# A transformer block on one core: values projected for two head groups at once, weights fetched per group, one tile pool for both stages

## The chip, the cores and the metric

The kernel runs on one core of a Trainium2 chip. The core has a matrix engine (TensorE, PE in the profile, with its weight loads shown apart as PEld), three engines for elementwise work (VectorE or DVE, ScalarE or ACT, GpSimd or POOL) and SyncE (SP), whose queue issues most transfers. SBUF is the on-chip memory that the engines read; PSUM is the accumulator that TensorE writes, used here as eight banks of 512 float32 per partition. The metric is the device time of one execution in microseconds, and lower is better.

## The reference

The input is x of 8 sequences x 1024 positions x 512 features in float32. Each sequence goes through attention with 16 heads of 32 features and then through a feed-forward part:

```python
qvk = (layernorm(h) @ Wqvk).reshape(b, s, 3, H, HD)       # 512 -> 3 * 512
q, v, k = qvk[:, :, 0], qvk[:, :, 1], qvk[:, :, 2]
scores = (einsum('bshi,bthi->bsth', q, k) + causal_mask) / sqrt(512)
wv = einsum('bsth,bthi->bshi', softmax(scores, axis=2), v)
x = x + layernorm(wv @ Wo)                                 # the attention's own input is layernorm(x)
hidden = layernorm(x) @ W1 + b1                            # 512 -> 2048
hidden = hidden + quantum_phase * w_imag * sin(theta + hidden * 0.1) * 0.1
x = x + layernorm(relu(hidden) @ W2 + b2)                  # 2048 -> 512
```

`softmax(scores, axis=2)` normalises over the key positions t. Its maximum over them is computed in full by the kernel.

## The kernel before

**Blocks and groups.** One sequence is one block b. A block's attention runs over four head groups g, each of four heads, so 128 columns of queries, keys and values. Then comes the feed-forward part (FFN). Everything is float32 but the maxima, which are split into bfloat16 parts; a float32 matmul shows as two records in the profile.

**One group.** `find_maxima` computes the scores once (L536) only for their row maxima: VectorE drains the PSUM banks with masked minima (L566, since queries carry a minus sign) on the diagonal tiles and with plain reductions (L554) elsewhere. The last two units of this, `MAX_LATE`, are run by `later(at)`, right ahead of the first two key units of the second part. The maxima are split by GpSimd (`split`), transposed on TensorE (the four bfloat16 transposes at L117) and copied to mT by ScalarE (L624). Then `weigh` goes over key units (`KEY_UNITS`): a matmul puts minus the maximum into PSUM (L642), the scores are computed again on top (L653), ScalarE takes the exponential (L668), and GpSimd clears the masked square (L672). `weighted_values` (L691) multiplies with the values one unit later, through `flush`.

**Fill.** TensorE executes in program order. The projections of the *next* group are a Python generator, `project_qkv(b, g)`, that `advance` moves a step at a time between the score units: a step is two matmuls of 512 columns for queries and keys (L437), or eight of 128 columns for values (L458) with one bank and one ScalarE copy (L466). `MAX_FILL` says how many steps follow each of the four runs of `find_maxima`; one more `advance(work)` stands behind the transposes of the maxima, one behind each of the first two key units (`at < 2`), and one at each of the last two. In group 2 the next block's normalised rows are also transposed there (`norm1`), and in group 3 the first half's output projection begins (`finish_block`, L857).

**FFN.** `feed_forward` runs eight steps of products with mixed (sums and differences of) W1 tiles (L949) and accumulates with W2 (L1033). The products "5", "4" and "6" read `mixed`, which GpSimd makes at L893 from the transposed rows. `load_w1(9)` and `load_w2(4)` keep tiles in flight on SP's queue.

**PSUM.** `psum` hands out banks in program order. It prefers the bank, or the pair of banks, that was released longest ago in that order (`done_at`); a tile that is not yet `drained` keeps its bank, and with it the pair that the bank belongs to, out of use. A score unit and a key unit take two pairs each, of the four. Whatever engine read the bank last is waited for by the matmul that writes it next.

**SBUF.** `wqvk_sb` (24 KB per partition) and `wo_sb` (8 KB) stay resident; queries and keys have a pool of 2 (`qkp`), values of 2 (`vp`), scratch of attention and FFN one of 8 (`pp`), W1 tiles 10 and W2 tiles 5. All allocations of a pool are in turn; a new tile waits for the last reader of the one whose place it takes.

Of the kernel before, what the change touches and what calls it, by code (L numbers as in the profile page):

```python
# [32 lines left out]
def kernel(  # L33
# [33 lines left out]
    qkp = ctx.enter_context(tc.tile_pool(name="qkp", bufs=2))  # L67
    vp = ctx.enter_context(tc.tile_pool(name="vp", bufs=2))
    pp = ctx.enter_context(tc.tile_pool(name="pp", bufs=8))
    tmp = ctx.enter_context(tc.tile_pool(name="tmp", bufs=5))  # L70
    small = ctx.enter_context(tc.tile_pool(name="small", bufs=4))
    w1p = ctx.enter_context(tc.tile_pool(name="w1p", bufs=10))
    w2p = ctx.enter_context(tc.tile_pool(name="w2p", bufs=5))
# [55 lines left out]
    wqvk_sb = const.tile([P, KC, 3 * D], F32, tag="wqvk", name="wqvk_sb")  # L129
    wo_sb = const.tile([P, KC, D], F32, tag="wo", name="wo_sb")  # L130
# [8 lines left out]
    for cols in (slice(0, P), slice(P, D)):  # L139
        for part in (0, 1, 2):  # L140
            of = slice(part * D + cols.start, part * D + cols.stop)
            nc.scalar.dma_start(wqvk_sb[:, :, of], wqvk_v[:, :, of])
        if cols.start == 0:
            for t in range(TPB, NT):
                load_x(0, t, nc.scalar)
# [41 lines left out]
    nc.scalar.dma_start(wo_sb, w_o.rearrange("(kc p) n -> p kc n", p=P))  # L187
# [45 lines left out]
    def w1_tile():  # L233
        return w1p.tile([P, 2, 2, P], F32, tag="w1", name="w1_t")
# [189 lines left out]
    def project_qkv(b, g):  # L424
# [3 lines left out]

        qk[b, g] = qkp.tile([P, 2, S], F32, tag="qk", name=f"qk_{b}_{g}")
        v[b, g] = vp.tile([P, NT, P], F32, tag="v", name=f"v_{b}_{g}")  # L430

        def queries_or_keys(n, half):
            pq = psum([P, HALF])
            c0 = 2 * n * D + g * P
            for kc in range(KC):
                in_order(
                    nc.tensor.matmul(  # L437
                        pq,
                        wqvk_sb[:, kc, c0 : c0 + P],
                        xnT[b, half][:, kc, :],  # L440
                        start=(kc == 0),
                        stop=(kc == KC - 1),
                    )
                )
                if kc == 1:
                    yield True
            dst = qk[b, g][:, n, half * HALF : (half + 1) * HALF]
            in_order(nc.scalar.activation(dst, pq, AF.Copy, scale=1.0 if n else -QSCALE))
            drained(pq)
            yield True  # L450

        def values(t0):
            pv = psum([P, 2, P])
            c0 = D + g * P
            for t in (t0, t0 + 1):
                for kc in range(KC):
# [4 lines left out]
                            wqvk_sb[:, kc, c0 : c0 + P],  # L461
# [4 lines left out]
            in_order(nc.scalar.copy(v[b, g][:, t0 : t0 + 2, :], pv))  # L466
            drained(pv)
            yield True

        yield from queries_or_keys(0, 0)  # L470
        yield from values(0)
        yield from queries_or_keys(1, 0)
        yield from queries_or_keys(0, 1)
        yield from queries_or_keys(1, 1)
        for t0 in (2, 4, 6):
            yield from values(t0)
# [13 lines left out]
    MAX_FILL = ((3, 2, 2, 2), (1, 2, 2, 2))  # L490
# [6 lines left out]
    def find_maxima(b, g, work, sums, more):  # L497
# [3 lines left out]
        t = qk[b, g]  # L501
# [23 lines left out]
        def run_unit(pieces):  # L525
# [4 lines left out]
            for i, kc in pieces:  # L530
                k0 = kc * HALF
                n = min(HALF, (i + 1) * P - k0)
                for j in range(HPG):
# [4 lines left out]
                            t[r, 0, i * P : (i + 1) * P],  # L538
                            t[r, 1, k0 : k0 + n],
# [57 lines left out]
        for n, (run, fill) in enumerate(zip(MAX_RUNS, MAX_FILL[g > 0])):  # L597
# [11 lines left out]
        advance(work)  # L609
# [18 lines left out]
    def weigh(b, g, c, keys, mT):  # L628


        t = qk[b, g]
# [3 lines left out]
        for kb in keys:  # L635
# [14 lines left out]
            for j in range(HPG):  # L650
# [4 lines left out]
                        t[r, 1, kb * P : (kb + 1) * P],  # L655
                        t[r, 0, q0 : q0 + n],
# [74 lines left out]
    def attention(b, wvT, after):  # L731
# [16 lines left out]
        def projections(g):  # L748
            if g + 1 < NG:
                return project_qkv(b, g + 1)  # L750
            if g + 1 == NG and b + 1 < B:
                return project_qkv(b + 1, 0)
            return iter(())

        work = projections(0)
        for g in range(NG):
            more, first = after(g)
# [3 lines left out]
            for c in range(2):  # L761
# [3 lines left out]
                for u, keys in enumerate(units):  # L765
                    later(at)
                    weights, placed = weigh(b, g, c, keys, mTs[c])
                    if at < 2:
                        advance(work)
# [6 lines left out]
                    if c and u == len(units) - 2:  # L776
                        finish(work)
                        work = projections(g + 1)
                    if c and u >= len(units) - 2:
                        advance(work)  # L780
# [42 lines left out]
            flush()  # L823
            if g == NG - 1:
# [4 lines left out]
        return more  # L829

    def finish_block(b, half, wvT, x2T, mixed):
# [21 lines left out]
        def project(t):  # L853
            y = psum([P, D])
            for kc in range(KC):
# [4 lines left out]
                        wo_sb[:, kc, :],  # L860
# [41 lines left out]
    def feed_forward(b, x2T, mixed, before, between):  # L902
# [22 lines left out]
        def load_w2(depth):  # L925
            while len(w2_ahead) < depth and w2_next[0] < 4 * STEPS:
                t = w2p.tile([P, D], F32, tag="w2", name="w2_t")
# [161 lines left out]
        for s in range(STEPS + 1):  # L1089
            if s == NSTEP:  # L1090
# [3 lines left out]
            for n in range(4):  # L1094
# [4 lines left out]
                advance(rest)  # L1099
                if s > 0:  # L1100
# [6 lines left out]
    first_norm, work = norm1_first(), project_qkv(0, 0)  # L1107
    advance(first_norm, TPB + 4)
    for _ in range(TPB):
# [3 lines left out]
    advance(work, 4)  # L1113
    prepare_parameters()
    finish(work)
    rest = iter(())
    for b in range(B):
        load_tables()
        wvT = [tp.tile([P, KC, HALF], F32, tag="t", name=f"wvT_{b}_{n}") for n in range(2)]
        x2T, mixed = {}, {}  # L1120

        def after(g, b=b, wvT=wvT, x2T=x2T, mixed=mixed, rest=rest):
# [10 lines left out]
            if g == NG - 1:  # L1133
                return finish_block(b, 0, wvT[0], x2T, mixed), len(KEY_UNITS[0]) + 1
            return iter(()), 0

        before = attention(b, wvT, after)
        rest = feed_forward(b, x2T, mixed, before, finish_block(b, 1, wvT[1], x2T, mixed))
# [44 lines left out]
```

## Time and profile before

| what | value |
|---|---|
| median of 3 runs | 3766.18 us (3761.59 to 3766.65) |
| the profiled execution | 3764.15 us, of which the span is 3762.4 us |
| TensorE busy | 3697.7 us, 98% of the span |
| granted TensorE clock, mean | 0.994 |
| one block (stretch 977 to 1441) | 464 us, TensorE busy 460.07 |
| DMA | 267.12 MB, mean 71 GB/s |

The profile is of one execution, so what is added up from its rows belongs to 3764.15 us and not to the median. A group of instructions is shown by its line, engine, operation and tiles; the numbers are busy time and the mean of one instruction. Matmuls overlap in the pipeline, so the mean of one is longer than the step from one start to the next; for what a stretch of matmuls costs, the chain of work that ended last is the better view, since each piece there lasts until the next begins. A wait is listed with what released it: total, number of times, longest.

### The profile page before, as it was taken

The numbers are of one execution on the slowest core, as the hardware profiler recorded it, in microseconds if no ns is written. First come the engines' busy times: TensorE is split into PE (matmuls) and PEld (weight loads), VectorE is DVE, ScalarE is ACT, GpSimd is POOL, SyncE is SP. The second block draws the span as 40 slices with busy tenths as digits, with TensorE's granted clock in tenths as the row PEclk, the third lists the DMA queues.
The fourth block names the chain that finished last, engine by engine and source line by source line (L and its number), as shares of the span: only waits on it lengthen the run. The fifth ranks groups of instructions, "written<-read, shape, count | busy, mean of one in ns | idle before, by whom it ended". The sixth has DMA issues, their size and how long they took to land.

```text
span 3762.4 us, 55976 instructions
## 1 busy us (share of the span) xinstructions
PE 3697.7 (98%) x21185; PEld 2062.4 (55%) x21185; DVE 2486.1 (66%) x5355; ACT 1417.1 (38%) x2704; POOL 650.7 (17%) x1204
## 2 busy tenths in 40 slices
PE   7999999999999999999999999999999999999998
PEld 4446655466554664446644466444664456654565
DVE  4866567666676666766577665776667765677655
ACT  3562135511465114651146411564115641156310
POOL 3212012120212102121022110221102211022200
PEclk9999999999999999999999999999999999999999
DMA  7003420044200442004420044100441003400132
GB/s 247 26 10 107 134 82 13 4 117 132 73 15 4 122 133 68 12 7 126 134 60 12 12 129 133 53 13 18 131 133 46 13 21 112 131 29 1 40 111 77
DMA packets 152909, 267.12 MB, mean 71 GB/s; under 512 B 16256, under 2 KB 27584, under 8 KB 152640
## 3 DMA queue, kind: packets, MB, share of 16 engines
q1 hardware_dynamic: 148368, 258.31, 23.2%
q10 hardware_dynamic: 4272, 5.24, 0.4%
q8 instruction: 167, 2.74, 0.3%
q14 instruction: 102, 0.84, 0.1%
HBM read 239.37 MB, written 24.12 MB: 70 GB/s over the span
## 4 chain that ended last, share of the span: by engine, by line
PE 95%; ACT 2%; DVE 1%; POOL 1%; DMA 0%; issue 0%; ACTq 0%; POOLq 0%; SPq 0%; DVEq 0%
PE banks L1033 23%; PE banks L949 20%; PE banks L437 12%; PE banks L536 8%; PE banks L691 7%; PE banks L653 7%; PE banks L458 7%; PE banks L857 6%; PE banks L642 3%; PE banks L117 2%; PE banks L706 1%; ACT w L668 1%; POOL mix L893 0%; ACT x2T L305 0%; DMA wqvk_sb<-in_L_attn_Wqvk_dram 0%
## 5 line engine op out<-in xcount | busy, mean ns | idle before, releaser
L1033 PE MATMUL banks<-w_t,hid 128*128 128x512 f32 x2048 | 915.5, 592 | 0.0
L668 ACT ACTIVATE w<-banks 128x1024 f32<-128x1024 f32 (+1 forms) x640 | 565.7, 936 | 291.9 <-PE banks L653 291.9
L1033 PEld LDWEIGHTS banks<-w_t,hid 128*128 128x128 f32 x2048 | 387.2, 190 | 393.0 <-issue 376.9
L720 DVE TENSOR_TENSOR w<-w 128x1024 f32<-128x1024 f32 (+3 forms) x400 | 408.6, 1062 | 200.8 <-PE banks L691 157.8
L566 DVE CUSTOM_DVE_ANT_0 es<-banks,mask 128x128 f32<-128x128 f32 (+3 forms) x1024 | 433.0, 486 | 104.6 <-PE banks L536 104.6
L437 PE MATMUL banks<-xnT,wqvk_sb 128*128 128x512 f32 x1024 | 481.6, 609 | 6.5 <-ACT xnT L305 6.5
L972 ACT ACTIVATE u<-u 128x1024 f32<-128x1024 f32 x128 | 135.3, 1057 | 903.9 <-DVE u L971 903.9
L949 PE MATMUL banks<-x2T,w_t 128*128 128x256 f32 x2048 | 473.6, 379 | 0.0
L949 PEld LDWEIGHTS banks<-x2T,w_t 128*128 128x128 f32 x2048 | 387.4, 190 | 127.9 <-issue 81.3
L672 POOL TENSOR_SCALAR_AFFINE_SELECT w<-w 128x256 f32<-128x256 f32 x512 | 278.4, 560 | 856.8 <-ACT w L668 814.0
L554 DVE TENSOR_REDUCE mx<-banks 128x1 f32<-128x512 f32 (+1 forms) x384 | 309.8, 862 | 102.0 <-PE banks L536 102.0
L949 PE MATMUL banks<-mix,w_t 128*128 128x256 f32 x1536 | 359.6, 384 | 15.4 <-POOL mix L893 15.4
L949 PEld LDWEIGHTS banks<-mix,w_t 128*128 128x128 f32 x1536 | 294.2, 192 | 86.3 <-issue 30.6
L653 PE MATMUL banks<-qk 32*128 32x512 f32 (+3 forms) x3072 | 330.6, 491 | 0.0
L437 PEld LDWEIGHTS banks<-xnT,wqvk_sb 128*128 128x128 f32 x1024 | 182.5, 190 | 245.1 <-issue 180.9
L691 PE MATMUL banks<-w,v 128*32 128x512 f32 (+3 forms) x3072 | 314.8, 495 | 1.0 <-POOL w L672 1.0
L536 PE MATMUL banks<-qk 32*128 32x512 f32 (+3 forms) x3072 | 313.5, 511 | 0.3 <-DVE mx L566 0.2
L586 ACT ACTIVATE es<-es,mx 128x512 f32<-128x512 f32 (+3 forms) x512 | 279.7, 551 | 2.1 <-DVE mx L566 2.1
L458 PEld LDWEIGHTS banks<-wqvk_sb,xnT 128*128 128x128 f32 x2048 | 239.0, 192 | 50.8 <-issue 23.6
L458 PE MATMUL banks<-wqvk_sb,xnT 128*128 128x128 f32 x2048 | 259.5, 280 | 0.0
L976 DVE SCALAR_TENSOR_TENSOR hid<-u,coef,hid 128x512 f32<-128x512 f32 x256 | 180.9, 749 | 109.7 <-ACT u L972 109.7
L857 PE MATMUL banks<-wo_sb,wvT 128*128 128x512 f32 x512 | 241.4, 612 | 3.2 <-DVE wvT L728 3.2
(110 smaller groups left out, 3173.4 us busy)
## 6 DMA issues: line engine op xcount, KB each, us to landing
w_t<-w_mixed SPq DMA_DIRECT2D x448, 256.0 KB, 2.7
w_t<-in_L_ffn_W_dram SPq DMA_DIRECT2D x256, 256.0 KB, 2.6
xin<-in_L_attn_h_dram SPq DMA_DIRECT2D x112, 256.0 KB, 3.5
out_dram<-x SPq DMA_DIRECT2D x64, 256.0 KB, 2.0
x<-in_L_attn_h_dram SPq DMA_DIRECT2D x60, 256.0 KB, 2.8
w_mixed<-w_t SPq DMA_DIRECT2D x28, 256.0 KB, 3.0
w_t<-in_L_ffn_W_dram SPq DMA_DIRECT2D x32, 128.0 KB, 2.9
wqvk_sb<-in_L_attn_Wqvk_dram ACTq DMA_DIRECT2D x3, 768.0 KB, 7.8
```

The source lines that it names most:

```text
L437: nc.tensor.matmul(pq, wqvk_sb[:, kc, c0 : c0 + P], xnT[b, half][:, kc, :], start=(kc == 0), stop=(kc == KC - 1),)
L458: nc.tensor.matmul(pv[:, t - t0, :], xnT[b, t // TPB][:, kc, (t % TPB) * P : (t % TPB + 1) * P], wqvk_sb[:, kc, c0 : c0 + P], start=(kc == 0),
L536: nc.tensor.matmul(scs[j // 2][:, j % 2, at : at + n], t[r, 0, i * P : (i + 1) * P], t[r, 1, k0 : k0 + n], start=True, stop=True,)
L554: nc.vector.tensor_reduce(out=mx[:, m], in_=sc[:, m, cols], op=ALU.min, axis=mybir.AxisListType.X,)
L566: nc.vector.tensor_tensor_reduce(out=es[:, m, cols], in0=sc[:, m, cols], in1=mask[:, HALF - n :], scale=1.0, scalar=FMAX, op0=ALU.add, op1 ...
L653: nc.tensor.matmul(sts[j // 2][:, j % 2, cols], t[r, 1, kb * P : (kb + 1) * P], t[r, 0, q0 : q0 + n], start=False, stop=True,)
L668: in_order(nc.scalar.activation(w[:, :, :width], st[:, :, :width], AF.Exp, scale=-1.0))
L691: nc.tensor.matmul(acc[r, HALF - n :], v[b, g][:, kb, r], weights[j // 2][:, j % 2, cols], start=first and k == 0, stop=last and k == len( ...
L720: in_order(nc.vector.tensor_add(t[:, :, q], t[:, :, q], w[:, :, cols]))
L857: nc.tensor.matmul(y, wvT[:, kc, t * P : (t + 1) * P], wo_sb[:, kc, :], start=(kc == 0), stop=(kc == KC - 1),)
L949: nc.tensor.matmul(bank[:, n, :], w[:, n, kc, :], moving[:, kc, :], start=first and kc == 0 and n == 0, stop=kc == 1 and n == 1, skip_grou ...
L1033: nc.tensor.matmul(ys[half, t], hids[s, 1 - n // 2][:, n % 2, t * P : (t + 1) * P], w, start=s % NSTEP == 0 and n == 0, stop=s % NSTEP == ...
```

## The change

- `project_qkv` becomes two generators. `project_queries_keys` has the query and key steps only. `project_values(b, pair)` projects the values of two groups at once: a matmul streams 256 columns of weights, and a step is four matmuls; after the first four (t == t0) the generator yields while the bank is still being filled, and after the second four come two ScalarE copies, one to each group's value tile.
- The value steps run behind the first two key units and at the last two of groups 0 and 1 (for the pair of groups 2 and 3), of group 3 (for the next block's first pair), and in the FFN's first step. Group 2 has none. `MAX_FILL` is two steps everywhere, and the `advance(work)` behind the transposes of the maxima is gone.
- The resident weights are gone. Query, key, value and output weights are fetched from DRAM for each block, in tiles of 2 KB per partition, from one pool `wp` of 20 that W1 and W2 tiles share.
- Queries, keys, values and scratch share one pool `pp` of 20 tiles.

```diff
-    qkp = ctx.enter_context(tc.tile_pool(name="qkp", bufs=2))
-    vp = ctx.enter_context(tc.tile_pool(name="vp", bufs=2))
-    pp = ctx.enter_context(tc.tile_pool(name="pp", bufs=8))
+    pp = ctx.enter_context(tc.tile_pool(name="pp", bufs=20))
-    w1p = ctx.enter_context(tc.tile_pool(name="w1p", bufs=10))
-    w2p = ctx.enter_context(tc.tile_pool(name="w2p", bufs=5))
+    wp = ctx.enter_context(tc.tile_pool(name="wp", bufs=20))
...
-    wqvk_sb = const.tile([P, KC, 3 * D], F32, tag="wqvk", name="wqvk_sb")
-    wo_sb = const.tile([P, KC, D], F32, tag="wo", name="wo_sb")
...
-    for cols in (slice(0, P), slice(P, D)):
-        for part in (0, 1, 2):
-            of = slice(part * D + cols.start, part * D + cols.stop)
-            nc.scalar.dma_start(wqvk_sb[:, :, of], wqvk_v[:, :, of])
-        if cols.start == 0:
-            for t in range(TPB, NT):
-                load_x(0, t, nc.scalar)
+    def fetch_queries_keys(b, g, queue=nc.sync):
+        for part in (0, 2):
+            w_of[b, g, part] = w_tile([KC, P], "wqk")
+            c0 = part * D + g * P
+            queue.dma_start(w_of[b, g, part], wqvk_v[:, :, c0 : c0 + P])
+
+    def fetch_values(b, pair, queue=nc.sync):
+        for k in (0, 2):
+            w_of[b, pair, "v", k] = w_tile([2, 2 * P], "wv")
+            c0 = D + 2 * pair * P
+            queue.dma_start(w_of[b, pair, "v", k], wqvk_v[:, k : k + 2, c0 : c0 + 2 * P])
+
+    def fetch_out():
+        out_w = []
+        for kc in range(KC):
+            out_w.append(w_tile([D], "wo"))
+            nc.sync.dma_start(out_w[kc], w_o[kc * P : (kc + 1) * P, :])
+        return out_w
+
+    fetch_queries_keys(0, 0, nc.scalar)
+    fetch_values(0, 0, nc.scalar)
+    for t in range(TPB, NT):
+        load_x(0, t, nc.scalar)
+    fetch_queries_keys(0, 1)
...
+    def project_values(b, pair):
+        groups = [2 * pair, 2 * pair + 1]
+        for g in groups:
+            v[b, g] = pp.tile([P, NT, P], F32, tag="p", name=f"v_{b}_{g}")
+        for t0 in range(0, NT, 2):
+            pv = psum([P, 2, 2 * P])
             for t in (t0, t0 + 1):
                 for kc in range(KC):
                     in_order(
                         nc.tensor.matmul(
                             pv[:, t - t0, :],
                             xnT[b, t // TPB][:, kc, (t % TPB) * P : (t % TPB + 1) * P],
-                            wqvk_sb[:, kc, c0 : c0 + P],
+                            w_of[b, pair, "v", kc - kc % 2][:, kc % 2, :],
                             start=(kc == 0),
                             stop=(kc == KC - 1),
                         )
                     )
-            in_order(nc.scalar.copy(v[b, g][:, t0 : t0 + 2, :], pv))
+                if t == t0:
+                    yield True
+            for n, g in enumerate(groups):
+                in_order(
+                    nc.scalar.copy(v[b, g][:, t0 : t0 + 2, :], pv[:, :, n * P : (n + 1) * P])
+                )
             drained(pv)
             yield True
...
-    MAX_FILL = ((3, 2, 2, 2), (1, 2, 2, 2))
+    MAX_FILL = (2, 2, 2, 2)
...
         mT = transpose_maxima(parts_q[0], nc.scalar.copy)
-        advance(work)
...
+            work = projections(g)
+            if g == 0:
+                fetch_values(b, 1)
+                values = project_values(b, 1)
+            elif g == NG - 1 and b + 1 < B:
+                values = project_values(b + 1, 0)
+            elif g == NG - 2 and b + 1 < B:
+                fetch_values(b + 1, 0)
...
                     if at < 2:
-                        advance(work)
+                        advance(values)
...
-                    if c and u == len(units) - 2:
-                        finish(work)
-                        work = projections(g + 1)
                     if c and u >= len(units) - 2:
-                        advance(work)
+                        advance(values)
...
+                if s == 0:
+                    advance(values)
```

The lines after the change, where the prediction names them: value projections L489 (before L458), scores L564 (L536), their minima L594 (L566) and reductions L582 (L554), minus the maxima L669 (L642), FFN products L984 (L949).

## The prediction

> **What bounds the kernel now.** I read the page's busy shares and chain, then the table of waits, then pieces of the chain inside one head group, then single rows where the change touches. The page:
>
> ```profile
> PE 3697.7 (98%) x21185; PEld 2062.4 (55%) x21185; DVE 2486.1 (66%) x5355; ACT 1417.1 (38%) x2704; POOL 650.7 (17%) x1204
> ...
> PE 95%; ACT 2%; DVE 1%; POOL 1%; DMA 0%; issue 0%; ACTq 0%; POOLq 0%; SPq 0%; DVEq 0%
> ...
> L458 PE MATMUL banks<-wqvk_sb,xnT 128*128 128x128 f32 x2048 | 259.5, 280 | 0.0
> ```
>
> TensorE (PE) is busy 98% and is 95% of the chain: what makes PE wait or stream longer is paid in full; work elsewhere is paid only where PE waits for it. The value projections are 2048 records (two per f32 matmul), never idle before. PE's waits of before:
>
> ```profile
> PE banks L949 <- POOL mix L893: 15.4, 8, 1.9
> PE banks L642 <- ACT w L668: 7.9, 33, 0.6
> PE banks L437 <- ACT xnT L305: 6.5, 1, 6.5
> ```
>
> (total us, times, longest.) All waits are small because projections fill them. The chain through the start of the weighing in block 3, group 1 (start, length, work):
>
> ```profile
> 1517.87 0.22 PE banks L117 x4
> 1518.10 1.84 PE banks L458 x16
> 1519.94 1.07 PE banks L536 x8
> 1521.01 0.22 PE banks L642 x4
> 1521.22 0.86 PE banks L653 x8
> 1522.08 1.98 PE banks L458 x16
> 1524.06 1.07 PE banks L536 x8
> ```
>
> Scores (L536), the product with minus the maxima (L642) and scores again (L653) follow value fills (L458) of 1.84 to 1.98 us. The change takes the first fill away and reshapes the second.
>
> **The change, part by part.** The sum is made against the profiled execution, 3764.15 us, which is 2.0 below the median of 3766.18. A change under about 0.2% (7.5 us) can't be told from none.
>
> 1. Streaming. A 128-column record takes 1.84/16 to 1.98/16, on the chain at 44.00 us 5.36/48 = 112 ns; a 256-column one 216 ns (L949 x16 on the chain at 1692.96 takes 3.45). 2048 x 112 = 229.4 us becomes 1024 x 216 = 221.2: **-8.2**. The built order has 11 more changes between full-height and quarter-height matmuls; a fill takes 1.84 to 1.98 where 16 x 112 is 1.79, so one change costs 0.05 to 0.19; at 0.09, **+1.0**.
>
> 2. The prologue. Before, ScalarE issues the big weight transfers ahead of its first copy, and PE waits for that copy (rows of the timeline: start, length, engine, ACTq being ScalarE's queue; in brackets the idle time before and what ended it):
>
> ```profile
> 12.08 4.51 ACTq L142 DMA_DIRECT2D wqvk_sb<-in_L_attn_Wqvk_dram  x2
> 19.65 0.40 ACTq L187 DMA_DIRECT2D wo_sb<-in_L_attn_Wo_dram  x1
> ...
> 23.48 3.78 PE L437 MATMUL banks<-xnT,wqvk_sb 128*128 128x512 f32 x4 [6.47 <-ACT xnT L305]
> ```
>
> ScalarE's table load comes at 20.08 and its four L305 copies at 21.38. After, it issues four 256 KB tiles and the four x tiles, then copies; the load and the copies can start some 9 us earlier (the 4.51 at 12.08 and the wo issue behind it are gone), with the first projection near 14.3 instead of 23.48: **-9.5** (-12 if all of it comes forward, -5 if the next tiles' normalisation is late instead; the 2.5 us idle at L117 in the same stretch is nearest).
>
> 3. The second key unit, the heart of it. Values now advance in half steps: after the first half (V4: four 256-column matmuls, 8 x 216 = 1.73 us) the generator yields with its PSUM bank still open, so of four bank pairs only three are in turn. The late score unit takes two, and the weighing that follows takes the third and one just written by the late unit: in the built order the third and fourth L642 matmul of 384 columns wait for the two single minimum reductions of that pair. Before, they waited for a value copy long done. The price, from the late unit's reductions:
>
> ```profile
> 1525.15 2.42 DVE L554 TENSOR_REDUCE mx<-banks 128x1 f32<-128x512 f32 x3 [1.59 <-PE banks L536]
> ```
>
> The scores start at 1523.99 in the timeline, so the reductions start 1.16 us after them; its two single parts release 0.70 and 1.31 us later, at 2.47 us after the scores' start. PE reaches the third L642 at about 1.0 to 1.05 (1.07 of scores on the chain): a stall of **1.43**. Behind it PE holds L653, the next V4 and L691; ScalarE's exponentials wait for L653, and VectorE for nothing new. Add 0.1 for L642 waiting for the copy of the transposed maxima, which had 1.84 us of fill over it and now has only 1.07 us of scores. It happens in groups 0 and 1 of eight blocks and group 3 of seven: 23 x 1.53 = **+35** (0 if reductions come earlier; 2.0 each, +46, if the whole pair's drain of 2.42 is waited for in part).
>
> 4. Group 2 has no value fill at all, only the next block's eight row transposes. Its second score unit came 5.0 us after the first (L536 at 1573.75 and 1578.75 in group 2 of this block); without 1.98 of fill VectorE's four masked minima (4 x 0.69 after 1.16) hold the banks 0.45 longer, the exponentials (0.97 each, two before the next L642) hold it some 0.9, and the transposes' banks wait twice some 0.5 for ScalarE's row copies of about 0.6: 2.3 each, x7 = **+16** (5 if only the first of these binds, 25 if the copies queue behind the exponentials). In the last block group 2 gets no fill at all: its group 3 shows that case today, from L117 at 3476.84 to L691 at 3485.21, 8.37 us for pieces that sum to 4.6 on the chain above: **+4**.
>
> 5. Group 0's first fill loses its values: the second score unit waits for VectorE's minima of the first. They ended at 1447.41, PE needed them at 1448.2; now 1.9 earlier: 1.1 x 7 = **+8** (0 to 9).
>
> 6. Weights per group: 28 MB more over 3764 us is 7.5 GB/s beside the page's 71, in 256 KB tiles that land in 2.6 to 3.5 us and are asked for a stage ahead on SP, past its FFN weights and x loads. Hidden by the FFN's PE work; a tile asked for too late would cost those 2.6 to 3.5. The one pool of 20 buffers adds no wait I can find on PE: **0**.
>
> 7. The clock. All blocks begin the FFN with a 1.9 us wait for the mix. In block 0 half clock follows, in block 1 it doesn't:
>
> ```profile
> 295.79 2.46 PE L949 MATMUL banks<-mix,w_t 128*128 128x256 f32 x8 [1.93 <-POOL mix L893]
> 298.05 4.87 PE L857 MATMUL banks<-wo_sb,wvT 128*128 128x512 f32 x8
> ...
> 759.69 1.99 PE L949 MATMUL banks<-mix,w_t 128*128 128x256 f32 x8 [1.92 <-POOL mix L893]
> 761.52 3.60 PE L857 MATMUL banks<-wo_sb,wvT 128*128 128x512 f32 x8
> ```
>
> From 295.79 to the next piece at 302.75 is 6.96, from 759.69 to 764.95 is 5.26: 1.7 us each, in seven blocks of eight. Which blocks pay depends on where the wait falls in windows of 3.4 us, which the change shifts; with about half of them paying I take **-5.6** (-12 to +2).
>
> 8. Group 3's V4 at the last two key units covers L642's 0.2 us waits: **-2**; the last block's half-clock stretch near 3475 shortens or grows: **+2**.
>
> Sum: -8.2 + 1.0 - 9.5 + 35 + 16 + 4 + 8 - 5.6 - 2 + 2 = +40.7, so **3804**.
>
> A rule that bears on part 7: the Trainium skill, "TensorE: Matmul & The Clock Gate", section "Why this matters for your kernels", asks for no idle gaps above about 3 us between bursts. By it neither the 1.9 us waits nor the new ones could cost clock, and part 7 would be 0, the sum 3810. The rows show half clock after 1.93, so the row decides.
>
> **The rivals.**
> - *The waits don't bind.* If the reductions of the late unit were already done, parts 3 to 5 fall and streaming, prologue and clock remain: 3764.15 - 8.2 + 1.0 - 9.5 - 5.6 = 3742. For it: VectorE idles 1.59 us just before; against: it idles because it waits for those very scores. It decides from a sum of new waits under 22.3/8 = 2.8 us a block; part 3 alone is 4.4. If just part 3 fell, 3770.
> - *The waits also cost clock.* Were each of 31 stalls followed by half clock at 1.7 us, +53: 3857. Against: 1.43 is shorter than 1.92, which was free in block 1.
> - *Weights come late.* Were each of 32 groups to wait 2.6 to 3.5 for its tiles: +83 to +112 on the forecast, 3887 or more; the point from which it decides anything is a tile landing later than the L437 or L458 that reads it. Against: DMA is busy 23% and tiles are asked for a stage ahead.
> - *It doesn't do what it says*: the built order holds 512 value matmuls of 256 columns for 1024 of 128; excluded.
>
> **How the numbers follow.** The forecast 0.85; no waits 0.06; part 3 alone missing 0.03; clock 0.04; late weights 0.02. The forecast's bounds: low with part 3 at 1.0 each (-12), part 4 at its low end in half (-5), clock at -12 (-6), partly together: 3784; high with part 3 at 2.0 (+11), part 4 at 25 (+9): 3826. That range holds the 0.8. Faster 0.06, same 0.03, slower 0.91.
>
> **What would show it.** In the changed profile: value records 1024 at 216 ns from start to start; a first projection near 14 us; a row of waits of L669 on the reduction L582, some 23 times 1.4 us; waits of L564 on the minima (L594) in groups 0 and 2; L984 still waiting 1.9 us for the mix. Wrong if L669 waits for nothing, if PE is idle on DMA, or if the granted clock falls in the key units.

## The result, and where the time went

The changed kernel takes 3809.73 us (median of 4; 3807.64 to 3814.33), against 3766.41 us before in the same comparison: a ratio of 1.0119 (95% interval 1.0102 to 1.0137). It is slower, and the forecast of 3804 us lies 5.7 us below it. The profiled execution took 3810.09 us, 45.9 more than that of before (3764.15); forecast against it were 40.7.

The page of the changed kernel, its busy shares, its chain by engine and the value projections:

```profile
PE 3724.7 (98%) x20161; PEld 2025.9 (53%) x20161; DVE 2472.7 (65%) x5355; ACT 1409.7 (37%) x2704; POOL 656.6 (17%) x1204
...
PE 91%; ACT 2%; DVE 2%; POOL 2%; DMA 1%; issue 1%; SPq 0%; POOLq 0%; ACTq 0%; DVEq 0%
...
L489 PE MATMUL banks<-wv,xnT 128*128 128x256 f32 x1024 | 250.5, 388 | 0.0
```

PE still reads 98% busy. The busy share can't show this change: the span grew with the busy time, and matmuls that stand waiting count in part as busy (the 512-column scores of L564 are the same work as before, and read 232.4 us for 218.5). What tells is the chain, where PE fell from 95% to 91%, and the table of waits (total us, times, longest):

```profile
PE banks L669 <- DVE mx L582: 20.5, 46, 0.6
PE banks L114 <- DVE xn L303: 15.8, 12, 8.6
PE banks L984 <- POOL mix L928: 15.4, 8, 1.9
PE banks L669 <- ACT w L695: 7.3, 32, 0.2
PE banks L718 <- POOL w L699: 4.2, 9, 0.6
```

The first row is new. It comes 46 times, which is twice in each of 23 groups, as forecast. Its 20.5 us is idle time alone; the chain in block 3, group 1 shows the whole price (start, length, work):

```profile
1539.73 0.22 PE banks L114 x4
1539.95 1.07 PE banks L564 x8
1541.03 0.26 PE banks L669 x4
1541.29 0.86 PE banks L680 x8
1542.15 1.93 PE banks L489 x8
1544.07 1.11 PE banks L564 x8
1545.18 0.11 DVE mx L582
1545.29 0.48 issue
1545.77 0.69 DVE mx L582
1546.46 0.04 issue
1546.50 0.32 PE banks L669
```

The transposes (L114) are followed at once by scores, one fill of 1.93 us (L489) comes later, and then the chain leaves PE: from 1545.18 to 1546.50 it runs over VectorE's reductions of the scores that began at 1544.07. In the kernel before, the scores at 1524.06 (1.07 us, in the prediction's chain) are followed without anything between by

```profile
1525.13 0.16 PE banks L642 x4
1525.30 0.65 PE banks L653 x8
```

Added up from start to start of the matmuls in the two traces, by line, the difference in the profiled spans comes to this:

| matmuls (line before, after) | us before | us after | difference |
|---|---|---|---|
| minus the maxima, 384 columns (L642, L669) | 11.5 | 46.4 | +34.9 |
| scores for the maxima, 512 columns (L536, L564) | 191.4 | 204.3 | +12.9 |
| weighted values (L691, L718) | 292.7 | 300.8 | +8.1 |
| scores for the weights (L653, L680) | 302.9 | 308.6 | +5.7 |
| value projections (L458, L489) | 249.3 | 239.3 | -10.0 |
| transposes, with the waits of the prologue (L117, L114) | 93.0 | 89.9 | -3.1 |
| output projection (L857, L892) | 237.2 | 235.1 | -2.1 |
| queries and keys, FFN products, sums, the time to the first matmul, the rest | | | -0.4 |
| sum | | | +46.0 |

### The profile page after: what moved, and what is told of

It is laid out like the page before. It is cut to its first block, busy times and chain, and to the rows that moved or that the text cites. A ratio compares the mean times of both kernels' runs of the same rounds, so it can differ in the third digit from the quotient of the medians.

```text
span 3808.4 us, 53672 instructions
## 1 busy us (share of the span) xinstructions
PE 3724.7 (98%) x20161; PEld 2025.9 (53%) x20161; DVE 2472.7 (65%) x5355; ACT 1409.7 (37%) x2704; POOL 656.6 (17%) x1204
## 4 chain that ended last, share of the span: by engine, by line
PE 91%; ACT 2%; DVE 2%; POOL 2%; DMA 1%; issue 1%; SPq 0%; POOLq 0%; ACTq 0%; DVEq 0%
PE banks L1068 23%; PE banks L984 20%; PE banks L457 11%; PE banks L564 7%; PE banks L680 6%; PE banks L718 6%; PE banks L489 6%; PE banks L892 6%; PE banks L669 3%; PE banks L114 1%; ACT w L695 1%; POOL w L699 1%; PE banks L733 1%; DVE mx L582 1%; POOL w_t L265 0%
## 5 line engine op out<-in xcount | busy, mean ns | idle before, releaser
L695 ACT ACTIVATE w<-banks 128x1024 f32<-128x1024 f32 (+1 forms) x640 | 566.9, 940 | 299.3 <-PE banks L680 299.3
L457 PE MATMUL banks<-xnT,wqk 128*128 128x512 f32 x1024 | 475.0, 607 | 0.7 <-ACT xnT L321 0.7
L984 PE MATMUL banks<-x2T,w_t 128*128 128x256 f32 x2048 | 473.9, 379 | 0.2 <-DVE u L1032 0.2
L594 DVE CUSTOM_DVE_ANT_0 es<-banks,mask 128x128 f32<-128x128 f32 (+3 forms) x1024 | 432.8, 485 | 47.7 <-PE banks L564 47.7
L984 PEld LDWEIGHTS banks<-x2T,w_t 128*128 128x128 f32 x2048 | 388.0, 190 | 122.7 <-issue 74.6
L582 DVE TENSOR_REDUCE mx<-banks 128x1 f32<-128x512 f32 (+1 forms) x384 | 309.6, 861 | 121.9 <-PE banks L564 121.9
L984 PE MATMUL banks<-mix,w_t 128*128 128x256 f32 x1536 | 360.0, 385 | 15.4 <-POOL mix L928 15.4
L984 PEld LDWEIGHTS banks<-mix,w_t 128*128 128x128 f32 x1536 | 294.7, 192 | 83.5 <-issue 27.3
L680 PE MATMUL banks<-q,k 32*128 32x512 f32 (+3 forms) x3072 | 336.5, 495 | 0.0
L564 PE MATMUL banks<-k,q 32*128 32x512 f32 (+3 forms) x3072 | 327.6, 514 | 0.3 <-DVE mx L594 0.2
L718 PE MATMUL banks<-w,v 128*32 128x512 f32 (+3 forms) x3072 | 317.8, 495 | 5.0 <-POOL w L699 4.2
L457 PEld LDWEIGHTS banks<-xnT,wqk 128*128 128x128 f32 x1024 | 184.4, 190 | 259.2 <-issue 206.6
L489 PE MATMUL banks<-wv,xnT 128*128 128x256 f32 x1024 | 250.5, 388 | 0.0
L892 PE MATMUL banks<-wo,wvT 128*128 128x512 f32 x512 | 239.3, 608 | 3.2 <-DVE wvT L755 3.2
L1032 DVE TENSOR_TENSOR u<-banks,p 128x512 f32<-128x512 f32 x128 | 88.1, 688 | 224.2 <-PE banks L984 224.2
```

The lines of the kernel that those rows point to most:

```text
L457: nc.tensor.matmul(pq, w[:, kc, :], xnT[b, half][:, kc, :], start=(kc == 0), stop=(kc == KC - 1),)
L489: nc.tensor.matmul(pv[:, t - t0, :], xnT[b, t // TPB][:, kc, (t % TPB) * P : (t % TPB + 1) * P], w_of[b, pair, "v", kc - kc % 2][:, kc % 2 ...
L564: nc.tensor.matmul(scs[j // 2][:, j % 2, at : at + n], queries[r, i * P : (i + 1) * P], keys[r, k0 : k0 + n], start=True, stop=True,)
L582: nc.vector.tensor_reduce(out=mx[:, m], in_=sc[:, m, cols], op=ALU.min, axis=mybir.AxisListType.X,)
L594: nc.vector.tensor_tensor_reduce(out=es[:, m, cols], in0=sc[:, m, cols], in1=mask[:, HALF - n :], scale=1.0, scalar=FMAX, op0=ALU.add, op1 ...
L680: nc.tensor.matmul(sts[j // 2][:, j % 2, cols], all_keys[r, kb * P : (kb + 1) * P], all_queries[r, q0 : q0 + n], start=False, stop=True,)
```

## The experiments

Times are medians, with the ratio to the kernel before in the same comparison (whose median was 3762 to 3764 there). Sums by group are added up from start to start in the profiled execution.

### Is it the open bank?

The first run closes the bank at every half step; the number and place of the fills stay. ScalarE's copies of the values become twice as many and half as large.

```diff
         for t0 in range(0, NT, 2):
-            pv = psum([P, 2, 2 * P])
             for t in (t0, t0 + 1):
+                pv = psum([P, 2 * P])
...
-                if t == t0:
-                    yield True
-            for n, g in enumerate(groups):
-                in_order(nc.scalar.copy(v[b, g][:, t0 : t0 + 2, :], pv[:, :, n * P : (n + 1) * P]))
-            drained(pv)
-            yield True
+                for n, g in enumerate(groups):
+                    in_order(nc.scalar.copy(v[b, g][:, t, :], pv[:, n * P : (n + 1) * P]))
+                drained(pv)
+                yield True
```

> The changed kernel, but each half step of values gets a PSUM bank of its own, drained at its end by two ScalarE copies, so that no bank is open when the generator yields. Theory (the open bank takes a pair out of use and makes the second key unit wait for the late unit's reductions): the four L669 matmuls of 384 columns in groups 0, 1 and 3 go from 1.71 us a group back to about 0.33, 23 x 1.38 = 31.8 off 3810, so 3776 to 3781. Rival (the wait comes from the missing or shorter fill, not from the bank): the wait stays and the time is 3806 to 3813.

Measured: 3769.70 us, ratio 1.0021 (1.0012 to 1.0030). The wait of L669 on the reduction is gone from the table. The chain at the same place:

```profile
1525.49 1.93 PE banks L489 x8
1527.42 1.07 PE banks L560 x8
1528.49 0.16 PE banks L665 x4
1528.65 0.65 PE banks L676 x8
```

The fill is as long as in the changed kernel (1.93), and the 384-column matmul takes 0.16 as before the change. In block 3 it falls from 1.71 to 0.33 or 0.34 us a group in groups 0, 1 and 3, over the run from 46.4 to 14.6: 31.8, to the decimal what was expected. The scores behind it give 3.4 more (0.13 a group, the rest in the last block), and the rest of the 38.6 by which the sums of the two profiles differ is in the FFN's products and output projections, where fewer blocks ran at half clock (below). The time lies 6 us below the expected range, by these last two. The profiled execution took 3772.10 us. So one open bank was 35 of the 46 us.

The second run leaves the bank open, and puts back a fill where the change had taken one away.

```diff
         mT = transpose_maxima(parts_q[0], nc.scalar.copy)
+        advance(values, 2)
...
-                    if c and u >= len(units) - 2:
-                        advance(values)
```

> The changed kernel, with a fill put back behind the transposes of the maxima: two half steps of values there (together one closed bank), taken from the last two key units of the same group. The bank is still open at the second key unit. Theory (the open bank): the wait of 1.38 a group stays; 0.1 to 0.2 a group around the transposes goes and as much comes back at the last two key units: 3804 to 3813. Rival (the missing fill): the wait goes and the time is 3776 to 3782.

Measured: 3852.40 us, ratio 1.0239 (1.0225 to 1.0253). This fits neither number. The waits, and the end of group 1 on the chain:

```profile
PE banks L719 <- POOL w L700: 21.7, 42, 0.8
PE banks L670 <- DVE mx L582: 20.5, 46, 0.6
```

```profile
1586.93 0.05 PE banks L670 x2
1586.98 0.32 PE banks L681 x7
1587.30 0.04 issue
1587.34 1.03 ACT w L696
1588.38 0.06 issue
1588.43 4.06 POOL w L700 x5
1592.49 0.04 issue
1592.53 1.17 PE banks L719 x8
```

The wait on the reduction is exactly what it was (20.5, 46 times), so the missing fill was not its cause, and the theory holds on the point that this run was to decide. The 43 us on top come from the other half of the edit: without fill at the last two key units the weighted values (L719) wait for GpSimd, which clears masked squares for 4.06 us in a row. In each group 0 and 1 the weighted values rise from 9.00 to 12.34 us: 16 x 3.35 = 54, of which some 11 came back, most of it in the value records (5.7) and the transposes of the maxima (2.1). I had put that cover at 0.1 to 0.2 us, from the waits that the kernel before shows there; those waits are small because of the fill.

### The wait in the FFN and the clock

```diff
             nc.scalar.copy(p1, one)
+            if s == 0:
+                advance(values)
             two = bank()
             product(two, s, "6", True)
```

> The changed kernel, with one half step of values (1.73 us of matmuls) moved in the FFN's first step from behind the products to between product 1 and product 6, where TensorE waits 1.9 us for the mix. Theory (that idle time is what makes the half clock follow): 7 x 1.7 to 1.9 of wait go and the half-clock windows of up to 7 blocks at 1.7 each with them: 3785 to 3792. Rival (half clock follows for another reason, so it stays): 3795 to 3799.

Measured: 3788.95 us, ratio 1.0070 (1.0056 to 1.0084), 20.8 less than the changed kernel. The timeline of the changed kernel at the FFN's start in block 3, then of this run:

```profile
1703.42 1.89 PE L984 MATMUL banks<-x2T,w_t 128*128 128x256 f32 x8
1707.23 3.08 PE L984 MATMUL banks<-mix,w_t 128*128 128x256 f32 x8 [1.92 <-POOL mix L928]
1710.11 4.24 PE L892 MATMUL banks<-wo,wvT 128*128 128x512 f32 x8
```

```profile
1694.12 1.89 PE L984 MATMUL banks<-x2T,w_t 128*128 128x256 f32 x8
1695.85 1.89 PE L489 MATMUL banks<-wv,xnT 128*128 128x256 f32 x8
1697.96 1.99 PE L984 MATMUL banks<-mix,w_t 128*128 128x256 f32 x8 [0.22 <-POOL mix L928]
1699.79 3.60 PE L892 MATMUL banks<-wo,wvT 128*128 128x512 f32 x8
```

The idle time falls from 1.92 to 0.22, and the product behind it, 3.08 us for eight records in the changed kernel, takes 1.99, and the output projection 3.60 for 4.24. In the changed kernel the granted clock is 0.50 from 1707.98 to 1711.39 us; six blocks have such a stretch at the FFN's start, and in this run none has. The theory that the idle time calls the half clock stands.

Which wait is followed by half clock can be read from the granted clock in the traces. These stretches last 3.41 us each, and every change of the clock in a run lies a whole number of such steps from the next (in the changed kernel the six start 471.04 us apart, 138 steps). Counted on in these steps, the six waits before them lie inside one step (from 0.68 to 2.93 us of its 3.41), and the two without half clock reach its end or cross it (1.51 to 3.43 and 2.52 to 4.44). Over all fourteen profiles, 47 of these 1.9 us waits lie inside one step and were followed by half clock, and 35 cross an edge and were not; only two, in the run with resident weights, lie inside within 0.05 us of an edge and were not either. The Trainium skill, "TensorE: Matmul & The Clock Gate", section "Why this matters for your kernels", sets the limit for idle gaps at about 3 us; here 1.92 us was enough where it fell inside one step.

### Group 0

```diff
             advance(work, fill)
+            if g == 0 and n == 0:
+                advance(values, 2)
```

> The changed kernel, with two half steps of values put behind the first run of maxima of group 0 (as before the change, where a value step stood there), taken from the last two key units of group 1. Theory (the second score unit of group 0 waits for VectorE's minima of the first): the 512-column score matmuls of group 0 fall from 6.99 to 5.8 us, 8 x 1.2 = 9.3 less, 3799 to 3803. Rival (the wait only moves to the next unit): 3807 to 3812.

Measured: 3816.11 us, ratio 1.0145 (1.0130 to 1.0160): slower, not faster. The mechanism was right: the 512-column scores of group 0 fell from 6.99 to 5.82 us. But the two half steps were taken from the last two key units of group 1, and there L720 rose from 9.00 to 12.35, the same 3.35 as above: 26.6 us were lost over the run for 8.4 won in the scores and some 9 more in the FFN, the value records and the queries and keys.

### The weights from DRAM

```diff
-            w_of[b, g, part] = w_tile([KC, P], "wqk")
-            queue.dma_start(w_of[b, g, part], wqvk_v[:, :, c0 : c0 + P])
+            w_of[b, g, part] = wqvk_sb[:, :, c0 : c0 + P]
+            if b == 0:
+                queue.dma_start(w_of[b, g, part], wqvk_v[:, :, c0 : c0 + P])
```

(the values' and the output's weights likewise)

> The changed kernel with the projection and output weights resident again (fetched once, in the first block), the weight pool at 15 and the scratch pool at 14. Everything on TensorE stays as it is. Theory (fetching costs nothing): 3806 to 3813. Rival (the 28 MB more, or their place on SP's queue, cost time): below 3802.

Measured: 3808.09 us, ratio 1.0122 (1.0107 to 1.0137), within 1.6 us of the changed kernel. In block 3 the four groups take 55.36, 55.16, 52.69 and 78.43 us against 55.37, 55.11, 52.62 and 78.43. In the groups fetching cost nothing. Most of what the two profiles differ by lies in the FFN, with the clock.

### Group 2

Two runs put values there. The first puts them at its first two key units, where I had placed most of the group's price:

```diff
-            elif g == NG - 1 and b + 1 < B:
-                values = project_values(b + 1, 0)
             elif g == NG - 2 and b + 1 < B:
                 fetch_values(b + 1, 0)
+                values = project_values(b + 1, 0)
...
-            if n >= (g > 0) * (len(MAX_RUNS) - 2):
+            if n >= (g > 0) * (len(MAX_RUNS) - 2 - (g == NG - 2)):
                 advance(more)
...
-                    if c and u >= len(units) - 2:
+                    if c and u >= len(units) - 2 and g != NG - 2:
                         advance(values)
```

> The changed kernel with the next block's row transposes begun one step earlier in group 2 and two half steps of values put into group 2, at its first two key units, taken from the FFN's first step. Theory (group 2 lost its cover, 2.95 us a block over scores, L669, transposes and weighted values): most of 7 x 2.95 = 20.6 comes back, but the open bank may bring a wait of up to 1.4 into this group too: 3790 to 3803. Rival (the group is bound by ScalarE's and VectorE's work, whatever fills): 3806 to 3813.

Measured: 3813.82 us, ratio 1.0138 (1.0123 to 1.0153). In sum nothing came back. In block 3 the 512-column scores and the row transposes of the group gave back 0.36 and 0.38 us. But L669 of 384 columns rose from 0.71 to 1.71 us: the open bank brought its wait along, at 60 waits of L669 on the reduction in place of 46. The weighted values rose from 10.39 to 11.25: the row transposes that had been begun earlier were missing at the last key unit, and on the chain GpSimd's selects (4.09 us at 1626.80) stand there instead.

After the runs above had shown what the last two key units need, the second puts the same two half steps there:

```diff
-            elif g == NG - 1 and b + 1 < B:
-                values = project_values(b + 1, 0)
             elif g == NG - 2 and b + 1 < B:
                 fetch_values(b + 1, 0)
+                values = project_values(b + 1, 0)
...
-                    if at < 2:
+                    if at < 2 and g != NG - 2:
                         advance(values)
```

> The changed kernel with two half steps of values put at the last two key units of group 2, taken from the FFN's first step; nothing else. Theory, formed after the fills taken from the last two key units of groups 0 and 1 cost 3.35 us a group in L718 (weighted values behind GpSimd's select): the weighted values of group 2 fall from 10.39 to about 9.0 us, 7 x 1.4 = 10 less, 3797 to 3803; the waits at the group's start (T, L564, L669, 1.3 us) stay. Rival (group 2's waits all come from its start): 3807 to 3812.

Measured: 3793.81 us, ratio 1.0082 (1.0067 to 1.0097), 16 less than the changed kernel. The weighted values of group 2 fell from 10.39 to 9.00 us as expected, 7 x 1.39 = 9.7; the waits at the group's start stayed (L669 and L564 unchanged within 0.1). The profile has some 6 us more off its FFN products and output projections, which is fewer blocks at half clock. The time came out below the expected range for that reason.

What remains at the group's start, in the chain of the changed kernel:

```profile
1596.41 0.93 PE banks L680 x8
1597.33 0.01 issue
1597.34 0.07 ACT w L695
1597.41 0.48 issue
1597.89 0.02 ACTq L321
1597.91 0.35 issue
1598.26 1.02 ACT w L695
1599.29 0.97 ACT xnT L321 x2
1600.26 0.04 issue
1600.30 0.32 PE banks L669
```

Here L669 waits for ScalarE's row copies (L321), which stand behind its exponentials (L695): the copies are queued work of the fill itself.

### The prologue by itself

```diff
-            nc.scalar.dma_start(wqvk_sb[:, :, of], wqvk_v[:, :, of])
+            if cols.start == 0:
+                nc.scalar.dma_start(wqvk_sb[:, :, of], wqvk_v[:, :, of])
...
-    nc.scalar.dma_start(wo_sb, w_o.rearrange("(kc p) n -> p kc n", p=P))
+    for part in (0, 1, 2):
+        of = slice(part * D + P, (part + 1) * D)
+        nc.sync.dma_start(wqvk_sb[:, :, of], wqvk_v[:, :, of])
+    nc.sync.dma_start(wo_sb, w_o.rearrange("(kc p) n -> p kc n", p=P))
```

> The kernel before, with only the order of its first transfers changed: the weights of groups 1 to 3 and the output weights are issued on SP's queue behind the parameters instead of on ScalarE's queue ahead of its first copies. Theory (ScalarE's issuing held up the first projection): first projection near 15.5 us instead of 23.5 and 7 to 9 us less, 3757 to 3760 against 3766. Rival (the transfers themselves or the rows' normalisation bound the start, or the gain is lost again in group 0): 3764 to 3767.

Measured: 3764.90 us, ratio 1.0003 (0.9994 to 1.0012): no difference. The first projection came at 14.28 and the first scores at 40.22 instead of 49.29, 9.1 earlier, and group 0 of block 0 then took 65.79 us instead of 56.32. The waits table has the row that gave it back, and GpSimd's timeline what it was doing (start, length, work, idle before):

```profile
PE banks L117 <- POOL parts_q L525: 7.8, 1, 7.8
```

```profile
64.23 1.26 POOL L253 TENSOR_TENSOR w_t<-w_t 128x512 f32<-128x512 f32 x1 [6.98 <-DMA w_mixed<-w_t]
65.58 1.26 POOL L255 TENSOR_TENSOR w_t<-w_t 128x512 f32<-128x512 f32 x1
66.91 2.60 POOL L253 TENSOR_TENSOR w_t<-w_t 128x512 f32<-128x512 f32 x2
69.47 0.22 POOL L518 TENSOR_TENSOR mx<-mx,rows 128x16 f32<-128x16 f32 x1
```

GpSimd splits the first maxima (L518) only when it has mixed the W1 tiles, which come to it through DMA (the row names the stores of mixed tiles; the last of the eight loads landed at 64.11). The second try keeps SP's queue as it was, and issues the weights on ScalarE's behind its copies of the first rows:

```diff
     finish(first_norm)
+    for part in (0, 1, 2):
+        of = slice(part * D + P, (part + 1) * D)
+        in_order(nc.scalar.dma_start(wqvk_sb[:, :, of], wqvk_v[:, :, of]))
+    in_order(nc.scalar.dma_start(wo_sb, w_o.rearrange("(kc p) n -> p kc n", p=P)))
```

> The kernel before, with the weights of groups 1 to 3 and the output weights issued on ScalarE's queue behind its copies of the first rows, so that SP's queue issues the W1 tiles as early as before. Theory (the first projection comes 8 us earlier, and in the run with these weights on SP the gain was lost because GpSimd's mixing of late W1 tiles held up the split of the first maxima): 3754 to 3759 against 3762. Rival (GpSimd's mixing of W1 ends at the same time whatever the queue, so that the first split waits anyway): 3760 to 3764.

Measured: 3761.98 us, ratio 0.9997 (0.9988 to 1.0006): no difference either. The time lies in the rival's range, but this run doesn't decide between the two expectations: GpSimd's wait is gone, and another took its place. ScalarE's queue was held up at its issues, and PE waited for ScalarE at the first scores (2.7 us at L533):

```profile
32.38 9.85 ACTq L1112 DMA_DIRECT2D wqvk_sb<-in_L_attn_Wqvk_dram  x3
46.68 0.42 ACTq L1113 DMA_DIRECT2D wo_sb<-in_L_attn_Wo_dram  x1
47.14 1.08 ACT L445 ACTIVATE qk<-banks 128x512 f32<-128x512 f32 x2 [14.18 <-DMA w_t<-in_L_ffn_W_dram]
```

The first row puts three issues together. Each takes only 0.38 us; they start at 32.38, 39.04 and 41.85. In the trace an issue waits on the semaphore that its own transfer will count up. The second, the third and that of the output weights start 0.02 us after an earlier transfer with the same semaphore has landed (39.02, 41.83 and 46.66), and all three of those are W1 transfers of SP's queue. So ScalarE was held not by the issuing but by transfers of another queue, as the bracket of the last row says. Before that, from 18.71 to 23.04, PE had waited 4.33 us for normalised rows.

In the changed kernel the gain held in the main: its first projection starts at 15.48, and GpSimd's split costs 2.1 us of wait at L114.

### All together, twice

The first sum of edits takes the closed bank, the fills in the FFN and in group 0, and values at group 2's first units, as written above.

> The changed kernel with four edits together: closed banks, the fill in the FFN's first step, the fill in group 0, and values in group 2. If the terms add (31.8 + 20 + 9.3 + 18 less): 3725 to 3740, faster than the kernel before. If they share the same idle time: 3745 to 3765.

Measured: 3769.99 us, ratio 1.0022 (1.0012 to 1.0031): above both expected ranges, and no better than the closed bank alone. Against the profile with closed banks, the FFN's products take 17.2 us less and the 512-column scores 10.3 less, but the weighted values 32.6 more, as their fill had been spent elsewhere.

The second gives half steps to the places where a wait was measured, and the FFN's products give up theirs but for the one in their wait. It has the closed banks too; `late_values` is the last half step of the pair begun in the block before, run in group 0:

```diff
+            if n == 0:
+                finish(late_values)
...
-            elif g == NG - 1 and b + 1 < B:
-                values = project_values(b + 1, 0)
             elif g == NG - 2 and b + 1 < B:
                 fetch_values(b + 1, 0)
+                values = project_values(b + 1, 0)
...
-                    if at < 2:
+                    if at < 2 and g != NG - 2:
                         advance(values)
...
             nc.scalar.copy(p1, one)
+            if s == 0:
+                advance(values)
...
-                if s == 0:
-                    advance(values)
```

> The changed kernel, values in closed banks, and each of a block's 16 half steps put where a wait was measured: group 0 behind its first run of maxima (the last half step of the pair begun in the block before), groups 0, 1 and 3 at the first two and last two key units, group 2 at its last two, and one in the FFN between product 1 and product 6. Theory (the terms add where each half step is taken from a place that it does not cover: the FFN's products): 31.8 + 3.4 for the bank, some 20 for the FFN wait with its clock, 1.2 x 7 = 8 for group 0 and 1.4 x 7 = 10 for group 2, of 3810: 3735 to 3745, faster than the kernel before at 3762. Rival (as with the four edits together, something else loses what these win): 3755 or more.

Measured: 3738.26 us, ratio 0.9932 (0.9919 to 0.9946): 0.7% faster than the kernel before, and 71 us below the changed kernel, with its wider values, its fetched weights and its pools. So a kernel with these three need not be slower; what cost was the open bank and the places of the fill.

The last run asks how much of that the wider values carry. It is the kernel before with one value step moved into the FFN's wait:

```diff
         mT = transpose_maxima(parts_q[0], nc.scalar.copy)
-        advance(work)
+        if g < NG - 1:
+            advance(work)
...
-                        finish(work)
+                        if g == NG - 1:
+                            values = work
+                        else:
+                            finish(work)
                         work = projections(g + 1)
...
             nc.scalar.copy(p1, one)
+            if s == 0:
+                finish(values)
```

> The kernel before, with one edit: the last value step of the next block's first group (eight matmuls of 128 columns, 1.8 us) moves from group 3 into the FFN between product 1 and product 6, and the fill behind the transposes of the maxima in group 3 is left out so that the other steps move up. If the best version's gain is the FFN wait and not the wider values: 7 x 1.7 of wait and up to 7 half-clock windows of 1.7 go, some 0.3 a block comes back in group 3: 3738 to 3748, like the best version's 3738. If the wider values carry it: 3755 or more.

Measured: 3742.50 us, ratio 0.9946 (0.9932 to 0.9959). That is 20 of the 25 us by which the best version beats the kernel before: the FFN's wait and its clock, without anything else of the change. No block runs at half clock after it any more. Between this run and the best version lie 4 us, which were not compared side by side, so what the wider values carry is not shown beyond that.

## Why the prediction was right, step by step

- **Streaming (1), -7.2 with the mode changes.** The value projections gave 10.0 from start to start. The mode changes were not separated from it. Queries and keys gave 2.5 behind the prologue (the split's wait below left out), which the sum doesn't have.
- **Prologue (2), -9.5.** Until the first scores, less the value work that moved there (7.2 us of value records before, 13.9 after), 42.1 became 32.9: -9.2. Then 2.3 was lost again in group 0 of block 0 to GpSimd's split, which the step had not named: -6.9. That the issues ahead of ScalarE's first copy held it up was right, and the first try at the prologue showed it (first projection at 14.28). But it was not the issuing: the issues in the row of 4.51 us take 0.45 and 0.39, the second starts at 16.20, when an x tile with its semaphore had landed (16.18), and the one of the output weights at 19.65, after a W1 tile of SP's queue (19.63).
- **Second key unit (3), 23 x 1.53 = +35.** Right in place, count and cause: 31.9 us in L669 (1.38 a group), 3.6 in the scores behind it, 2.2 in the transposes of the maxima and 0.7 in L564, together 38.3. The run with closed banks took out 31.8 + 3.4.
- **Group 2 (4), 7 x 2.3 = +16.** Measured 2.94 in blocks 1 to 6 and 2.4 in block 0, together 20.1, and partly elsewhere. At the start it is 0.38 in L669, 0.51 in L564, 0.23 in L680 and 0.43 in the transposes; the prediction had 0.45, 0.9 and two waits of 0.5. The step that failed is the last of these, "the transposes' banks wait twice some 0.5": the largest piece, 1.39, is in the weighted values at the end of the group, behind GpSimd's select, which the step doesn't name; the run with values at the last two key units took it back whole. In the last block it was 2.3, not 4. Its +4 was read from a stretch of 8.37 us in which the granted clock was 0.70, so half clock made that stretch long, and not the missing fill alone.
- **Group 0 (5), +8.** Measured 1.21 on the 512-column scores in each block but the first, which has none: 8.5. The table of waits shows next to none of it (0.2 us on L594), though the prediction named such a row as a sign; it shows as 16 records of L564 that take 3.16 us on the timeline (at 1466.61) where they took 2.00 before (at 1447.22).
- **Weights (6), 0.** The resident run shows 0 in the groups.
- **Clock (7), -5.6.** Six blocks of eight ran into half clock at the FFN instead of seven, so about -1.7; the FFN in all gave 1.1. The prediction had the rule (where the wait falls in the steps of 3.4 us) but not the places; this term had the right bounds and no better.
- **Cover (8), -2 and +2.** Group 3's cover came to 0.17 in the sums (L706, L733) and 0.22 in the weighted values, 2.6 us in all. The last block's half clock near its end grew from 10.24 to 13.65 us, but its group 3 took only 0.13 more. The reading of the last two key units was wrong in size where it mattered: the fill there covers 3.35 us of a group, as the two runs that took it away found.

That the sum came within 5.3 us of the profiled difference (45.9 for 40.7) is in part luck. Above their terms came the clock by 4.5, group 2 by 4.1, the second key unit by 3.3, the prologue by 2.6 and group 0 by 0.5, together 15; below them streaming by 2.8, the cover by 2.6, queries and keys by 2.5 and the last block by 1.7, together 9.6. The largest term was right by its mechanism, and the range would have held without the luck. (The two terms of its upper end add to 3825, not 3826.)

The rival that the waits don't bind fell with the 46 waits; that they also cost clock did too, since no block shows half clock in groups 0 to 2, or in group 3 of blocks 0 to 6; late weights fell with the resident run.

## What to carry to other kernels

A generator that yields with a PSUM bank half filled holds that bank, and with it the pair, through whatever is issued in between; where an allocator deals out the rest in order, the next user gets a bank that was written a moment ago, and its reader is on the path. Fill is a budget: list the places where a wait shows once the fill is gone, not the waits that show while it is there, and move fill only from places that need none. Look for the longest idle stretch of the bounding engine first; here one step of 1.8 us in each block's 1.9 us wait was worth more than the wider matmuls.

## What the runs showed of the hardware that was not expected

- A wait of 1.92 us of TensorE is dear when it lies inside one step of 3.41 us of the clock: half clock followed in 47 of 49 such cases, at about 1.7 us each in the kernel before. With the wait down to 0.22 us in the run with that one edit, the half clock after it is gone.
- GpSimd's select on 128x256 elements took about 0.4 to 1.1 us each, and five in a row lay on the chain for 4.06 us, though the engine is busy only 17% of the span.
- Issuing a transfer of 768 KB took a queue 0.38 to 0.53 us. On ScalarE's queue three of them were spread over 9.85 us, the second and third held until a transfer of SP's queue with the same semaphore had landed; on SP's queue, in the first try at the prologue, the same three were through in 1.53 us.
